# The last inverse-Haar pieces of two channel chunks tied behind the joins of the inverse stage, in half pieces

## The chip, the cores and the metric

The kernel runs on one core of a Trainium2 chip. The metric is the device time of one execution in microseconds (us). The core's engines are PE (TensorE, matrix products), DVE (VectorE), ACT (ScalarE), POOL (GpSimd) and SP (SyncE, which issues transfers). The page also has PEld, PE's loading of weights, which overlaps PE's products.

## The reference, cut to what matters

The input is four images (batches) of 64 channels with 256 x 256 points. Four layers follow each other. Layers 0, 1 and 3 are long convolutions with a filter that is a product of a row filter and a column filter, plus the input times a bias for each channel:

```python
k = jnp.einsum('ijk,imk->ijmk', hx, hy)[0]
...
y = jnp.fft.irfft2(u_f * k_f, s=(fft_size, fft_size))[..., :L, :L]
out = y + x * bias[:, None, None]
```

Layer 2 transforms each channel with a two-dimensional Haar transform, mixes the channels with soft thresholds, transforms back and adds its input:

```python
f1 = haar2d(x)
acc = jnp.zeros_like(f1[:, :conv_w.shape[1]])
for i in range(v.shape[0]):
    f3 = f1 * v[i]
    f4 = jnp.einsum('bchw,oc->bohw', f3, conv_w[i])
    f5 = jnp.sign(f4) * jax.nn.relu(jnp.abs(f4) - tau[i])
    acc = acc + f5
y = haar2d(acc, inverse=True)
return y + x
```

## The kernel before

A separable convolution of a channel is two matrix products with triangular Toeplitz matrices, one for the columns and one for the rows (`contract`, lines 262 to 266, four matmuls a product). For each batch b there are three kinds of work.

`convolutions` runs layers 0 and 1 for the 64 channels, one channel a tick: product a0, copy by ACT (line 279), product y0, residual sum by DVE (line 296), the same again for a1 and y1, and then the forward Haar transform. Its results go to memory, as coefficients (`coef`) and as row sums and differences (`keep`).

`mixing` runs 64 groups of four Haar rows: matmuls (line 453) into PSUM, scaling by DVE and ACT (lines 472 and 477), the soft threshold (lines 481 to 492), and a sum into the large tile `z` (line 498). `z` holds a whole batch after the mixing: 128 partitions, then four chunks of 16 channels, 128 Haar rows (slots), and four values for each channel.

`inverse` transforms back and runs layer 3. It begins three ticks after the 64 ticks of mixing, at the tick called `start`, and takes one channel a tick: `fetch` (ACT, line 538) copies the channel out of `z`, `rows` (PE, lines 545 and 546) transforms its rows into one of two PSUM buffers, `join` (DVE, lines 564 to 572) adds the row sums and differences in one operation (line 567) and writes the sum and the difference of the halves (lines 570 and 571) into a tile `u`. Product a3, its copy by ACT, product y3, residual sum by DVE (line 296) and the transfer of the output follow from `u`. In batches 0 to 2 every third channel (2, 5, 8 and so on) is put off: its `u` goes to memory and its layer 3 runs during the mixing of batch 3.

The inverse transform along the other axis is done in place in `z`. For chunk 0 it is a product with a Haar matrix (`halves` and `cols`, lines 549 to 562), in the first 16 ticks. For chunks 1 to 3 DVE does it by levels: `level` (lines 306 to 310) calls `halve` (lines 301 to 304), a subtraction (line 303) and a second operation (line 304), over pairs of slots. Level n has n pairs of slots of 64 values; levels 32 and 64 are cut into pieces of 16 pairs, which are operations of 128 x 1024. So each chunk has seven such pieces: one of level 16, two of level 32 and four of level 64. Piece (3, 64, 2) below is chunk 3, level 64, third piece; it needs the level before it and the mixing groups that write its slots, and `fetch` of the chunk's first channel (16 times the chunk's number) needs all pieces of the chunk.

Each step is put at a time in ticks by hand (`at`, and the table `PLACE`); all steps are then written into the program in the order of these times. The scheduler of the framework places each engine's instructions in this order of preference, but takes an instruction of a later time first where the engine would be free in its plan and the data are there. An order that it must keep is given with `add_manual_dep`. Such an order between two instructions of one engine needs no semaphore.

The pieces of chunk c (1 to 3) are written at `start + 16 (c - 1)` and the ticks after it (lines 583 to 591): (2, 64, 3) at `start + 28`, (3, 32, 0) and (3, 32, 1) at 34 and 36, (3, 64, 0) to (3, 64, 3) at 38, 40, 42 and 44.

## Time and profile before

| | us |
|---|---|
| Median of three runs | 2873.04 |
| Lowest and highest of the three | 2872.15, 2877.78 |
| The profiled execution | 2873.81 |
| Span of its instructions | 2871.9 |

The busy times on the page are unions of the instructions' times. A matmul's end is modelled and consecutive matmuls overlap, so PE's idle time says more than its busy time. The 40 slices of the page are 71.8 us each:

```profile
DVE  4555558999999779999999769999999779999985
PEclk9999999999999999999999999999999999999999
```

The digits are the busy share of a slice in tenths. DVE's slices of 9 are the mixing stages, and the pairs of lower digits between them are the inverse stages of batches 0, 1 and 2. Joins (line 567) of batch 0 run from 873.9 us on, those of batch 1 from 1530.4, of batch 2 from 2182.5 and of batch 3 from 2648.0. In batch 0, join 16 starts at 932.1, join 28 at 964.5 and join 40 at 996.2.

### The profile page before, as it was taken

To read this page: it belongs to the slowest core of one execution; us is meant where nothing else is said; L and a number is where in the kernel's file an instruction comes from. 1 tells how busy PE (TensorE), PEld (TensorE's weight loads), DVE (VectorE), ACT (ScalarE), POOL (GpSimd) and SP (SyncE) were. 2 spreads that over 40 slices of the span, in tenths; PEclk is the share of its full clock that TensorE was granted. 3 is DMA by queue.
4 is the path that set the end of the run, shared out by engine and by line. 5 is a ranking of instruction groups with operands and counts; after the bars stand their busy time and mean duration, and the time that the engine had idled before them with its cause. 6 is when DMAs were issued, how large, how long until landed. Compare 5 with 4: busy or idle time off the path is not lost.

```text
span 2871.9 us, 52418 instructions
## 1 busy us (share of the span) xinstructions
PE 2822.6 (98%) x16594; PEld 2553.8 (89%) x16594; DVE 2492.5 (87%) x4240; ACT 2078.6 (72%) x4941; POOL 334.0 (12%) x644
## 2 busy tenths in 40 slices
PE   9999999999998999999999999999999999999999
PEld 8899998888887998998888898998888998888998
DVE  4555558999999779999999769999999779999985
ACT  2333348999985658989986658999995659998554
POOL 0111111122121001221211001121121000000000
PEclk9999999999999999999999999999999999999999
DMA  6877787676676986777777976777777988777786
GB/s 195 249 229 233 230 237 219 207 211 204 204 212 220 284 248 199 214 212 213 208 212 236 295 247 195 216 212 215 211 208 232 301 267 237 228 238 213 223 241 199
DMA packets 599382, 649.77 MB, mean 226 GB/s; under 512 B 48481, under 2 KB 517060, under 8 KB 598980
## 3 DMA queue, kind: packets, MB, share of 16 engines
q1 hardware_dynamic: 537012, 578.61, 68.3%
q10 hardware_dynamic: 62096, 67.82, 6.7%
q8 instruction: 134, 2.20, 0.3%
q14 instruction: 140, 1.15, 0.1%
HBM read 426.77 MB, written 219.48 MB: 225 GB/s over the span
## 4 chain that ended last, share of the span: by engine, by line
PE 46%; DVE 12%; ACT 5%; issue 3%; DMA 2%; POOL 0%; SPq 0%; ACTq 0%; DVEq 0%
PE pa L265 11%; PE py L265 11%; PE px L453 6%; PE pa L266 5%; PE py L266 5%; PE pw L545 3%; ACT f L477 3%; DVE mag L492 2%; DVE y L296 2%; DVE mag L488 2%; PE pw L546 2%; DMA t<-pad 1%; PE pz L385 1%; DVE z L498 1%; ACT mag L481 1%
## 5 line engine op out<-in xcount | busy, mean ns | idle before, releaser
L265 PE MATMUL py<-t,a 128*128 128x256 f32 x3072 | 922.4, 382 | 12.1 <-ACT a L279 11.2
L279 ACT COPY a<-pa 128x512 f32<-128x512 f32 x768 | 479.9, 625 | 500.4 <-PE pa L266 455.2
L477 ACT ACTIVATE f<-px,vt 128x64 f32<-128x64 f32 x2816 | 613.1, 369 | 100.6 <-DVE f L472 99.8
L266 PEld LDWEIGHTS py<-t,a 128*128 128x128 f32 x3072 | 583.4, 190 | 79.3
L266 PE MATMUL py<-t,a 128*128 128x128 f32 x3072 | 590.0, 274 | 0.0
L265 PEld LDWEIGHTS py<-t,a 128*128 128x128 f32 x3072 | 497.2, 191 | 53.8 <-ACT a L279 21.6
L453 PE MATMUL px<-wb,f 128*128 128x256 f32 x2048 | 487.6, 380 | 7.6 <-ACT f L477 7.6
L453 PEld LDWEIGHTS px<-wb,f 128*128 128x128 f32 x2048 | 369.0, 190 | 50.1 <-ACT f L477 10.5
L355 POOL TENSOR_TENSOR sd<-less 128x128 f32<-128x128 f32 (+4 forms) x320 | 190.2, 594 | 1859.7 <-DVE less L354 1478.3
L538 ACT COPY zc<-z 128x512 f32<-128x512 f32 x256 | 281.8, 1104 | 108.6 <-PE pw L546 100.1
L488 DVE TENSOR_TENSOR mag<-mag,vt 128x1024 f32<-128x1024 f32 x256 | 311.8, 1218 | 12.7 <-ACT mag L481 12.1
L265 PE MATMUL pa<-t,y 128*128 128x256 f32 x1024 | 309.0, 384 | 8.5 <-DVE y L296 5.5
L492 DVE SCALAR_TENSOR_TENSOR mag<-mag,f 128x1024 f32<-128x1024 f32 x256 | 311.8, 1219 | 0.0
L265 PE MATMUL pa<-t,x 128*128 128x256 f32 x1024 | 305.9, 380 | 1.8 <-DMA t<-pad 1.8
L481 ACT ACTIVATE mag<-f 128x1024 f32<-128x1024 f32 x256 | 296.0, 1156 | 2.7 <-DVE z L498 0.4
L378 DVE TENSOR_TENSOR sp<-sd,sp 128x512 fp32r<-128x512 f32 x256 | 178.5, 697 | 128.8 <-ACT sp L373 127.5
L484 ACT ACTIVATE f<-f 128x1024 f32<-128x1024 f32 x256 | 285.9, 1117 | 3.5
L265 PE MATMUL pa<-t,u 128*128 128x256 f32 x772 | 233.2, 384 | 6.7 <-ACT w L552 2.8
L296 DVE SCALAR_TENSOR_TENSOR y<-x,bsb,py 128x512 f32<-128x512 f32 x256 | 189.9, 742 | 45.5 <-PE py L266 45.3
L266 PEld LDWEIGHTS pa<-t,y 128*128 128x128 f32 x1024 | 194.5, 190 | 26.4
L266 PEld LDWEIGHTS pa<-t,x 128*128 128x128 f32 x1024 | 194.6, 190 | 26.3
L296 DVE SCALAR_TENSOR_TENSOR y<-y,bsb,py 128x512 f32<-128x512 f32 x256 | 189.5, 740 | 26.0 <-PE py L266 25.6
(72 smaller groups left out, 4378.5 us busy)
## 6 DMA issues: line engine op xcount, KB each, us to landing
t<-pad SPq DMA_DIRECT2D x767, 256.0 KB, 4.1
x<-in_x SPq DMA_DIRECT2D x256, 256.0 KB, 3.7
coef<-co SPq DMA_DIRECT2D x256, 256.0 KB, 3.1
f<-coef SPq DMA_DIRECT2D x256, 256.0 KB, 3.2
r<-keep SPq DMA_DIRECT2D x256, 256.0 KB, 4.0
out_y<-y ACTq DMA_DIRECT2D x193, 256.0 KB, 4.2
keep<-sums SPq DMA_DIRECT2D x256, 128.0 KB, 2.9
keep<-sd SPq DMA_DIRECT2D x256, 128.0 KB, 2.8
```

The costliest lines, as they stand in the source:

```text
L265: nc.tensor.matmul(ps[:, m, :], src[:, 0, m * P : (m + 1) * P], t[:, ::-1], start=True, stop=False)
L266: nc.tensor.matmul(ps[:, m, P:], src[:, 1, m * P : (m + 1) * P], t[:, : P - 1 : -1], start=False, stop=True)
L279: nc.scalar.copy(a, s["p" + new])
L296: nc.vector.scalar_tensor_tensor(y, s[res], bsb[:, layer, c : c + 1], s["p" + new], ALU.mult, ALU.add)
L355: engine.tensor_tensor(t[:, :, :, half:length], v[..., 0], v[..., 1], ALU.subtract)
L453: nc.tensor.matmul(ps[:, q, h, :], f[:, q, h * P : (h + 1) * P], wb.rearrange("p r n -> p (r n)"), start=True, stop=True,)
L477: nc.scalar.mul(f4[:, j], px[:, j], scale(g, 0)[:, j : j + 1])
L481: nc.scalar.activation(mag, st[g]["f4"], AF.Abs)
L484: nc.scalar.activation(st[g]["f4"], st[g]["f4"], AF.Sign)
L488: nc.vector.tensor_sub(mag, mag, over(g, 1, 16))
L492: nc.vector.scalar_tensor_tensor(mag, mag, 0.0, st[g]["f4"], ALU.max, ALU.mult)
L538: nc.scalar.copy(a.rearrange("p h k i -> p (h k) i"), z[:, c // 16, :, :, c % 16].rearrange("p i x -> p x i"))
```

## The change

A table `LATE` names pieces by batch: seven in batch 0, four each in batches 1 and 2, none in batch 3. A piece in the table is cut into two halves of eight pairs (operations of 128 x 512), written at the two ticks that the table gives, and the first operation of each half may not be placed ahead of the first operation (line 567 before) of the join that was written last before it; a half at tick k so goes behind the join of channel k - 1. In batches 0 to 2 the pieces of chunk 3 that are not in the table are written 17 ticks earlier than before (`start + 15` in place of `start + 32`). All other pieces stay where they were.

```diff
--- before.py
+++ after.py
@@ -82,6 +82,21 @@
     "l add": 3.47,
 }
 
+LATE = (
+    {
+        (2, 64, 3): (21, 23),
+        (3, 32, 0): (18, 19),
+        (3, 32, 1): (25, 27),
+        (3, 64, 0): (28, 29),
+        (3, 64, 1): (31, 32),
+        (3, 64, 2): (34, 35),
+        (3, 64, 3): (37, 38),
+    },
+    {(2, 64, 3): (21, 23), (3, 64, 1): (24, 26), (3, 64, 2): (28, 31), (3, 64, 3): (34, 37)},
+    {(2, 64, 3): (21, 23), (3, 64, 1): (24, 26), (3, 64, 2): (28, 31), (3, 64, 3): (34, 37)},
+    {},
+)
+
 INV_2PI = float(np.float32(1.0 / (2.0 * math.pi)))
 MAGIC = float(1.5 * 2.0**23)
 
@@ -298,16 +313,20 @@
 
         return [product, residual]
 
-    def halve(even, odd):
-
-        nc.vector.tensor_sub(odd, even, odd)
+    behind = [None]
+
+    def halve(even, odd, stay=False):
+
+        first = nc.vector.tensor_sub(odd, even, odd)
+        if stay and behind[0] is not None:
+            tc.add_manual_dep(first.ins, behind[0].ins.name, order, reason="not ahead of the joins")
         nc.vector.scalar_tensor_tensor(even, even, 2.0, odd, ALU.mult, ALU.subtract)
 
-    def level(n, chunk, begin=0, count=None):
+    def level(n, chunk, begin=0, count=None, stay=False):
 
         count = n if count is None else count
         v = z.rearrange("p n s x c -> p n s (x c)")[:, chunk].rearrange("p (j e s) x -> p j e s x", e=2, s=P // 2 // n)
-        halve(v[:, begin : begin + count, 0, 0, :], v[:, begin : begin + count, 1, 0, :])
+        halve(v[:, begin : begin + count, 0, 0, :], v[:, begin : begin + count, 1, 0, :], stay)
 
     def butterfly():
 
@@ -564,7 +583,7 @@
         def join(c):
             ps = st[c]["pw"]
             t = io.tile([P, 2, 2, P], F32, name=f"t_{b}_{c}", tag="res", bufs=BUFS["res"])
-            nc.vector.scalar_tensor_tensor(t, st[c]["r"], 0.5, ps, ALU.mult, ALU.add)
+            behind[0] = nc.vector.scalar_tensor_tensor(t, st[c]["r"], 0.5, ps, ALU.mult, ALU.add)
             u = io.tile([P, 2, S], F32, name=f"u_{b}_{c}", tag="y", bufs=BUFS["y"])
             v = u.rearrange("p m (w e) -> p m w e", e=2)
             nc.vector.tensor_add(v[:, :, :, 0], t[:, 0], t[:, 1])
@@ -576,19 +595,25 @@
 
         along = start - groups - 3
 
-        def when(tick, n, chunk, *span):
-            at(tick + PLACE["level"], lambda _: level(n, chunk, *span), 0)
+        def when(tick, n, chunk, *span, stay=False):
+            at(tick + PLACE["level"], lambda _: level(n, chunk, *span, stay=stay), 0)
 
         at(along + 11 + PLACE["level"], lambda _: butterfly(), 0)
         for chunk in range(1, 4):
             turn = start + 16 * (chunk - 1)
             for n in (1, 2, 4, 8):
                 when(along + 12 + 3 * chunk if b + 1 < B else turn, n, chunk)
+            if chunk == 3 and b + 1 < B:
+                turn = start + 15
             when(turn + 1, 16, chunk)
-            for i in range(2):
-                when(turn + 2 + 2 * i, 32, chunk, 16 * i, 16)
-            for i in range(4):
-                when(turn + 6 + 2 * i, 64, chunk, 16 * i, 16)
+            for n in (32, 64):
+                for i in range(n // 16):
+                    tick = LATE[b].get((chunk, n, i))
+                    if tick is None:
+                        when(turn + n // 16 + (n == 64) * 2 + 2 * i, n, chunk, 16 * i, 16)
+                    else:
+                        for j in range(2):
+                            when(start + tick[j], n, chunk, 16 * i + 8 * j, 8, stay=True)
 
         for c in range(C):
             for name, stage in zip(("sooner", "early", "fetch", "rows"), (sooner, early, fetch, rows)):
```

## The prediction

> **What bounds the kernel now.** I read the busy line first, then the busy time by stretch around the inverse stage, then the waits of PE there, then the order of VectorE's instructions at the longest wait.

> ```profile
> PE 2822.6 (98%) x16594; PEld 2553.8 (89%) x16594; DVE 2492.5 (87%) x4240; ACT 2078.6 (72%) x4941; POOL 334.0 (12%) x644
> ```

> PE, the matrix engine, is busy nearly all the time, so only its remaining idle time and slow stretches can be won. By stretch (columns: length; busy PE, weight loads, DVE, ACT, POOL, with counts; PE clock granted, DMA share, GB/s):

> ```profile
> 840.00:937.00 97.00, 87.35 (x525) 77.66 (x524) 94.43 (x156) 55.31 (x90) 10.02 (x20) 0.98 0.71 221
> 932.20:936.50 4.30, 4.30 (x16) 3.82 (x17) 2.83 (x6) 0.59 (x1) 0.00 (x0) 0.60 0.95 308
> 936.00:961.00 25.00, 24.93 (x167) 23.10 (x167) 18.32 (x35) 14.34 (x18) 0.00 (x0) 0.99 0.84 266
> 961.00:993.50 32.50, 32.49 (x213) 29.38 (x212) 24.56 (x47) 21.12 (x28) 0.00 (x0) 1.00 0.96 296
> 1591.00:1613.00 22.00, 21.26 (x140) 19.20 (x139) 15.45 (x30) 13.56 (x18) 0.00 (x0) 1.00 0.90 292
> 1613.00:1644.00 31.00, 30.99 (x204) 28.05 (x203) 23.75 (x46) 19.53 (x26) 0.00 (x0) 1.00 0.96 296
> 2648.00:2746.00 98.00, 97.13 (x630) 89.65 (x630) 97.47 (x162) 51.87 (x69) 0.00 (x0) 1.00 0.74 223
> ```

> The first two lines are batch 0 where mixing ends and the inverse stage begins (joins 0 to 16): DVE is full (94.43 of 97.00) and PE idles 97.00 - 87.35 = 9.65 us. Right after (joins 17 to 39) PE idles 0.08 us and DVE has room: 25.00 - 18.32 = 6.68 and 32.50 - 24.56 = 7.94 us. Batch 1 has 6.55 and 7.25 us of room at the same joins. What PE waits for, in 840 to 937:

> ```profile
> PE pa L265 <- issue: 2.1, 1, 2.1
> PE pw L545 <- ACT zc L538: 2.0, 1, 2.0
> PE py L265 <- ACT a L279: 1.7, 2, 1.5
> PE pw L545 <- DVE w L553: 1.5, 1, 1.5
> PE pa L265 <- DVE y L296: 1.4, 1, 1.4
> PE pa L265 <- DVE u L571: 0.6, 2, 0.3
> PE pa L265 <- PE pw L546: 0.3, 1, 0.3
> ```

> The first is put down to "issue"; DVE's order shows the cause, and PE's timeline the end of the wait:

> ```profile
> 926.56 0.68 DVE L567 SCALAR_TENSOR_TENSOR t<-r,pu 128x512 f32<-128x512 f32 x1
> 927.16 1.21 DVE L303 TENSOR_TENSOR z<-z 128x1024 f32<-128x1024 f32 x1
> 928.29 0.41 DVE L570 TENSOR_TENSOR u<-t 128x256 f32<-128x256 f32 x1
> 928.63 0.41 DVE L571 TENSOR_TENSOR u<-t 128x256 f32<-128x256 f32 x1
> 928.96 1.21 DVE L304 SCALAR_TENSOR_TENSOR z<-z 128x1024 f32<-128x1024 f32 x1
> 930.10 0.68 DVE L567 SCALAR_TENSOR_TENSOR t<-r,pu 128x512 f32<-128x512 f32 x1
> ```
> ```profile
> 932.20 0.67 PE L265 MATMUL pa<-t,u 128*128 128x256 f32 x2 [2.14 <-issue]
> ```

> A level piece stands inside join 14 (L303 between L567 and L570) and its second half ahead of join 15, which ends at 932.10; 0.10 us later PE, idle since 930.06, goes on. L303 of the large shape runs eleven times in that stretch and never after 927.2 in this stage, although the last seven pieces are written at ticks 33 to 44: pieces are placed wherever DVE is free in the planned order. In batches 1 and 2 they have all run by the first join; there PE waits only this around it (1493 to 1560):

> ```profile
> PE pa L265 <- ACT w L552: 1.4, 1, 1.4
> PE pw L545 <- DVE w L553: 0.7, 1, 0.7
> ```

> **The change part by part.**

> Moved: 7 pieces in batch 0, 4 each in batches 1 and 2. A large op occupies DVE from 927.16 to 928.29, 1.13 us; the other from 928.96 to 930.10, 1.14; a piece is 2.27 us. Seven are 15.9 us, seven of the last eight of those eleven by written order (ticks 28 and 34 to 44), taken out of a stretch with 97.00 - 94.43 = 2.57 us of DVE room.

> Gain in batch 0. Of the waits I count those that a late DVE can make: 2.1 + 2.0 + 1.5 + 1.4 + 0.6 + 0.3 = 7.9 us; not the 1.7 behind ACT's copy. The 2.0 behind ACT's fetch is the doubtful one. Then the clock: 0.60 over the 4.30 us after the longest wait loses 0.4 x 4.30 = 1.7 us. Together 9.6. Batches 1 and 2, whose DVE holds no pieces after the first join, still lose 1.4 + 0.7 = 2.1 there, so I take 9.6 - 2.1 = 7.5 us. Bounds: 0 (the waits have other causes) and 9.6.

> [...]

> Gain in batches 1 and 2. The last pieces there run at 1527.48 and 1529.29 on DVE, directly ahead of the first join at 1530.43, for which PE waits 1.4 us; 2.27 us less brings that join earlier by more than the wait. The 0.7 is a queue of the same DVE work. 2.1 us each. Bounds: 0, and 2.1 + 2.1 (in the mixing stretch 1057 to 1493 PE waits 1.6 us for DVE's residual sums and 0.5 for ACT's copy). The rest of DVE's relief in mixing I cost at nothing, because PE is busy 433.22 of 435.60 us there: PE's own work hides it.

> Added: 30 instructions. A half op is 128x512; the nearest rows are L378 (same shape, 0.68 us, next start 0.61 later at 1515.70) and L567 above (next start 0.60 later). So a half piece is 1.20 us, a piece 2.40, 0.13 more than now, 15 x 0.13 = 2.0 us of DVE over the program, inside the room below.

> [...]

> Cost at ticks 18 to 38. A half tied at tick k goes behind join k - 1. Batch 0: five (18 to 25) are 6.0 us into 6.68 of room; nine (27 to 38) are 10.8 us into 7.94: DVE is 2.9 us over, and since joins feed PE within 0.1 us (row above) I let PE lose all 2.9. What is late next: join, product a3, then the rows, for which there are two PSUM buffers. The stretch after tick 39 (5.86 us of room in 26.5) lets DVE catch up, but not PE. Batches 1 and 2: four halves, 4.8 us, into 6.55 and four into 7.25: they fit, and I take 0.5 us each for joins that a half stands inside. Bounds for each half: 0 and its full 1.20 us on PE's path, so 0 to 36 us in all; the nearest row is batch 3 (2648 to 2746), where whole pieces stand between joins, DVE is busy 97.47 of 98.00 and PE loses only 0.87. So near the low end.

> The tie itself: an order on one engine, no semaphore. Behind a tied op in DVE's queue stand that join's two sums, the next join and residual sum; PE's a3 and ACT's output transfer wait for these. No transfer moves in any queue. The last half of chunk 3 comes at tick 38 and the first fetch (L538) of that chunk at 48, ten ticks of over 2 us: hidden; were DVE later than that, ACT would wait. Chunk 3's earlier untied pieces only change priority: 0. Batch 3: unchanged.

> Sum: batch 0 -7.5 + 2.9 = -4.6; batches 1 and 2 2 x (-2.1 + 0.5) = -3.2; together -7.8. The profiled execution took 2873.8 us (span 2871.9), 0.8 over the median of 2873.04; 2873.8 - 7.8 = **2866.0 us**.

> **Rivals.**

> A, the stall moves along (faster by too little). Every tied half stands inside its join, as L303 does at 927.16, and delays u by 0.6 us; in each group of three channels one is deferred and one join feeds PE with some 0.1 to 0.3 us to spare, so about 13 joins lose 0.4: 5.2 us in place of the two 0.5, on top of 2.9. 2866.0 + 4.2 = 2870.2. For: the row at 927.16. Against: at 979.09 L378 stands inside a join (L570 at 978.75, L571 at 979.69), and PE waits 0.2 us in all from 936 to 1057.

> B, slower: the rotation join, a3, rows breaks under the halves as it does now under whole pieces. Then seven pieces cost at ticks 18 to 38 what they cost now, 9.6, against the gain of 7.5: +2.1; and four pieces cost 9.6 x 4/7 = 5.5 in batches 1 and 2 against 2.1: +3.4 each. 2873.8 + 8.9 = 2882.7. It decides once DVE is over 0.97 busy at those joins. For: 10.8 us into 7.94. Against: batch 3's row, and DVE's share after the change at batch 1's joins 20 to 39, (15.45 + 23.75 + 9.6) / 53 = 0.92.

> C, more: all waits bounded above vanish. 9.6 + 2 x 4.2 = 18.0 less the cost of 3.9: 2859.7. For: DVE is the releaser of most. Against: some are ACT's.

> D, the tie does not do what it says: the pieces before the tied ones move up, into the freed DVE time, and the waits stay; 2873 us. Against: only four of the eleven are left.

> **How the numbers follow.** Forecast 0.50, own range 2860 to 2871 (batch 0's gain 9.6 or its cost doubled); A 0.15; B 0.18; C 0.13; D 0.04. About 0.2%, 5.7 us, can be told from no change here: faster means under 2867.3. Faster: 0.40 of the forecast, C, 0.01 of A, 0.54. Within: 0.10 of the forecast, 0.13 of A, D, 0.27. Slower: B and 0.01 of A, 0.19. The range 2856 to 2880 leaves out the far part of C and the upper half of B, some 0.14.

> **What will show it.** Right: DVE's large L303 ops gone between joins 1 and 15 of batch 0, PE's idle time in that stretch down from 9.65 to 2 or 3 us, no 0.60 clock; half-size ops between joins 17 and 38; DVE near 1.0 in batch 0 at joins 27 to 39 with some 3 us of PE idle time; the 1.4 us ahead of the first join gone in batches 1 and 2. Wrong: new waits of pa for u above 4 us in a batch (A, B), or the waits of joins 0 to 16 still there without the pieces (their cause was ACT or PSUM buffers).

## The result, and the profile after

| | before | after |
|---|---|---|
| Median, six runs each, us | 2873.24 | 2858.89 |
| Lowest and highest, us | 2872.15, 2877.78 | 2858.58, 2860.41 |
| The profiled execution, us (span) | 2873.81 (2871.9) | 2858.95 (2857.1) |

The ratio is 0.995 (95% interval 0.9938 to 0.9962): 14.4 us faster. Timed again (e5), the ratio was 0.997 (0.9958 to 0.9981), 9.9 us between the medians of 2872.23 and 2862.32. Both intervals end below 1.

The line of busy times of the changed kernel:

```profile
PE 2820.0 (99%) x16594; PEld 2552.1 (89%) x16594; DVE 2492.0 (87%) x4270; ACT 2076.4 (73%) x4941; POOL 329.1 (12%) x644
```

The sums are those of before; DVE has the 30 added instructions and no more time. In what follows an inverse stage runs from the last mixing matmul of its batch to the first of the next. The stretches of batch 0's inverse stage, cut at joins 17 and 40, in the kernel before (columns: length; busy PE, weight loads, DVE, ACT, POOL; PE clock, DMA share, GB/s):

```profile
839.50:933.70 94.20, 84.55 (x514) 75.20 (x514) 93.48 (x155) 55.22 (x90) 10.02 (x20) 1.00 0.71 220
933.70:996.20 62.50, 62.43 (x404) 57.05 (x404) 46.40 (x89) 37.74 (x48) 0.00 (x0) 0.98 0.91 284
```

and the same stretches in the changed kernel, with the rest of the stage:

```profile
837.60:925.20 87.60, 83.70 (x522) 75.80 (x520) 78.82 (x142) 55.80 (x91) 9.09 (x20) 1.00 0.76 232
925.20:986.10 60.90, 60.18 (x391) 54.30 (x390) 59.64 (x116) 37.65 (x48) 0.00 (x0) 1.00 0.90 283
986.10:1048.10 62.00, 62.00 (x423) 57.97 (x422) 45.59 (x89) 32.37 (x40) 0.00 (x0) 1.00 0.92 290
```

Up to join 17 DVE has 14.7 us less to do, the stretch is 6.6 us shorter, and PE's idle time falls from 9.65 to 3.90 us. From there to join 40 DVE is now full (59.64 of 60.90), yet PE idles only 0.72 us. PE's waits in the changed kernel, first up to join 17, then to join 40:

```profile
PE py L280 <- ACT a L294: 1.7, 2, 1.5
PE pw L564 <- ACT zc L557: 1.2, 1, 1.2
PE pw L564 <- ACT w L571: 1.0, 1, 1.0
```
```profile
PE pw L564 <- DVE t L586: 0.4, 1, 0.4
PE pw L564 <- ACT zc L557: 0.2, 1, 0.2
```

Of the waits that were shown before, the one of 2.1 us behind a join, the 1.5 for DVE's halves and the 1.4 for a residual sum are gone; the 1.7 for ACT's copy is as it was. Of the 2.0 us behind ACT's fetch 1.2 are left, and a wait of 1.0 us for ACT's copy `w` (line 571) is new. A half piece among the joins (lines 586, 589 and 590 are the join; 320 and 323 the piece; 311 the residual sum; 397 part of the forward transform):

```profile
960.08 0.69 DVE L586 SCALAR_TENSOR_TENSOR t<-r,pw 128x512 f32<-128x512 f32 x1
960.69 0.69 DVE L320 TENSOR_TENSOR z<-z 128x512 f32<-128x512 f32 x1
961.29 0.42 DVE L589 TENSOR_TENSOR u<-t 128x256 f32<-128x256 f32 x1
961.63 0.42 DVE L590 TENSOR_TENSOR u<-t 128x256 f32<-128x256 f32 x1
961.96 0.69 DVE L397 TENSOR_TENSOR sp<-sd,sp 128x512 fp32r<-128x512 f32 x1
962.57 0.68 DVE L323 SCALAR_TENSOR_TENSOR z<-z 128x512 f32<-128x512 f32 x1
```

It does stand inside its join, and holds L589 until 961.29; without a piece, L570 of before started 0.72 us after its L567 (943.15 and 943.87 in the trace of before), so here by 960.80. The price is 0.49 us.

### The profile page after: what moved, and what is told of

It reads as the page before. It is cut to its first block, busy times and chain, and to the rows that moved or that the text cites. A ratio compares the mean times of both kernels' runs of the same rounds, so it can differ in the third digit from the quotient of the medians.

```text
span 2857.1 us, 52492 instructions
## 1 busy us (share of the span) xinstructions
PE 2820.0 (99%) x16594; PEld 2552.1 (89%) x16594; DVE 2492.0 (87%) x4270; ACT 2076.4 (73%) x4941; POOL 329.1 (12%) x644
## 5 line engine op out<-in xcount | busy, mean ns | idle before, releaser
L472 PEld LDWEIGHTS px<-wb,f 128*128 128x128 f32 x2048 | 369.0, 190 | 50.5 <-ACT f L496 10.8
```

Source lines behind the costliest of these rows:

```text
L472: nc.tensor.matmul(ps[:, q, h, :], f[:, q, h * P : (h + 1) * P], wb.rearrange("p r n -> p (r n)"), start=True, stop=True,)
```

## The experiments

The stage lengths from the traces say more than the times, because they repeat. In us; a mixing stage is the stretch between two inverse stages:

| kernel | inverse 0 | inverse 1 | inverse 2 | first stage |
|---|---|---|---|---|
| before | 217.9 | 216.8 | 209.2 | 440.1 |
| before, again (e1) | 217.5 | 213.5 | 209.8 | 438.3 |
| after | 210.5 | 212.3 | 208.4 | 437.7 |
| after, again (e2) | 210.6 | 212.4 | 208.4 | 442.0 |
| after, a third time (e5) | 210.5 | 213.4 | 208.4 | 439.4 |
| batch 0 only (e3) | 210.7 | 214.1 | 209.3 | 437.3 |
| batches 1 and 2 only (e4) | 217.5 | 212.3 | 208.4 | 441.4 |
| halves, not tied (e6) | 212.9 | 214.7 | 209.8 | 439.0 |
| whole pieces, tied (e7) | 216.3 | 213.8 | 210.4 | 442.2 |
| tied behind the join's last op (e8) | 211.7 | 212.7 | 208.9 | 437.5 |
| two more pieces moved (e9) | 212.5 | 212.3 | 208.4 | 440.8 |
| quarters (e10) | 212.5 | 212.1 | 208.3 | 439.4 |
| all pieces of batches 0 to 2 halved (e11) | 211.0 | 212.5 | 208.8 | 440.5 |
| batch 3's halved too (e12) | 210.7 | 212.4 | 208.6 | 437.8 |

Some expectations speak of "PE's loss over steady pace": the sum of how much later than at full pace each matmul starts after the one ahead of it (full pace is taken as 216 ns after a matmul of 256 columns, 110 after one of 128; the medians from start to next start in the trace of before are 216 and 111). It holds PE's idle time and some 3 us a stretch of matmuls that start late by little.

**e1 and e2, both kernels again.** No edit.

> The kernel before, unchanged, profiled a second time. In its first profile PE lost 2.6 us at 118 us (a Toeplitz load in the first stage) and 2 x 1.2 us in batch 1's inverse stage, where ACT's issue of the output transfer took 1.8 and 2.0 us; the changed kernel's profile has 0.9 us and none. Theory (these belong to each execution, not to the change): in this second profile they are elsewhere or gone, and the span stays within 2870 to 2876 us. Rival (they belong to the planned order of the kernel before, and the change removed them): they come again at the same places with the same lengths.

> The changed kernel, unchanged, profiled a second time. Theory (chance waits): first stage 437 to 441 us, batch 1's inverse stage 212 to 216 us, depending on where transfers are slow; batch 0's inverse stage stays at 210.5 us and DVE is again 0.93 to 1.00 busy at joins 16 to 39 of batch 0 with PE idle about 1 us. Rival (all differences are the change's): every stage repeats within 0.3 us.

The kernel before took 2867.75 us this time, below the range given. The long issues of the output transfer in batch 1 were gone (its stage 213.5 in place of 216.8 us), with one of 1.17 us in batch 2, and PE's wait at 118 us had become one of 1.4 us at 116. In the changed kernel the first stage took 442.0 us in place of 437.7 (I had said up to 441), and its inverse stages repeated within 0.1. So the first stage and the long issues vary with the execution, in either kernel: over all profiles the first stage lies between 437.3 and 442.2 us, and issues of the output transfer of more than 1 us came three times in the first profile of before, once in e1, three times in e6, once in e7, once in a third profile of the changed kernel (e5) and never in its first two. That the change makes the long issues rarer is not excluded: of the five profiles whose batches 1 and 2 have no tied halves (before, e1, e3, e6, e7) four hold at least one, of the nine others one. What surely belongs to the change lies in the inverse stages.

**e3 and e4, one part alone.** In e3 the table and the new `turn` hold for batch 0 only, in e4 for batches 1 and 2 only:

```diff
-            if chunk == 3 and b + 1 < B:
+            if chunk == 3 and b == 0:
```

> Only batch 0's pieces are moved, tied and halved. Theory: the gain of each batch lies in its own inverse stage and they add: batch 0's stage 217.9 to 210.5 us, so about 2866 us (2873.2 - 7.4). Rival (much of the total comes from batches 1 and 2): 2869 us or more.

> Only the pieces of batches 1 and 2 are moved, tied and halved. Theory (batch 1's long waits for output transfers are chance, the change gives 0.8 to 1.2 us a batch, as its profile shows in batch 2): 2871 to 2872 us. Rival (the change removes them too): 4.5 + 0.8 = 5.3 us, 2868 us. My forecast's term for these two batches was 3.2 us, 2870 us.

e3: 2863.66 us, ratio 0.9974 (0.9964 to 0.9984). e4: 2866.36 us, ratio 0.9986 (0.9977 to 0.9994); before in the same session 2870.26. Each kernel has the short stages of the batches that it changes and the long ones of the others, so the gains add: 7.0 us in batch 0 (217.5 to 210.5), 1.2 to 1.8 in batch 1 (213.5 and 214.1 to 212.3) and 0.8 to 1.4 in batch 2, together 9 to 10 us. The medians of e4 say 3.9 us where the stages say 2 to 3; its interval (1.7 to 6.6 us) holds both.

**e5, the changed kernel timed again.** No edit.

> The changed kernel again, timed. By stage the change is worth 6.5 us in batch 0 and 1.4 and 1.1 us in batches 1 and 2, 9.0 to 9.5 us; the rest of the 14.4 us measured first is waits that come and go with the execution. Theory: ratio 0.9965 to 0.997, some 9.5 us. Rival (the change also makes the chance waits rarer, as in the first six runs of it, which lay within 1.8 us): 14 us again, ratio 0.995.

Ratio 0.997 (0.9958 to 0.9981), 9.9 us by the medians: the theory. The interval reaches from 5.5 to 12.1 us, so 14 us again is out, but a part of the rival (rarer waits) is not. The first measurement's 14.4 us holds some 4 to 5 us that the stages don't show as the change's. In the first pair of profiles 2.4 us are the first stage and 3.3 batch 1's stage with its two long issues (216.8 in place of 213.5); that its six runs fell so is not explained further.

**e6, halves without the tie.**

```diff
-                            when(start + tick[j], n, chunk, 16 * i + 8 * j, 8, stay=True)
+                            when(start + tick[j], n, chunk, 16 * i + 8 * j, 8)
```

> The changed kernel without the ties: the same half pieces at the same ticks, free to be placed earlier. The planned order puts them at joins 0 to 22 of batch 0 and at joins 0 and 1 of batches 1 and 2. Theory (where the work stands sets the time, not its size or its written tick): batch 0's inverse stage 215 to 218 us, batches 1 and 2 213.5 and 209.3 as before, 2869 to 2873 us. Rival (halving alone relieves the joins, because a half holds a join by 0.6 instead of 1.2 us): batch 0 at 212 us or less, 2865 us.

The number of my theory fell: the halves ran up to join 22 of batch 0, as planned, and its stage took 212.9 us, 4.6 us less than with whole pieces (217.5 in e1). The rival's 212 us was missed by 0.9. 2864.43 us, ratio 0.9972 (0.9962 to 0.9982), which the time alone can't tell from the changed kernel. The stretches up to join 17 and to join 40:

```profile
837.90:929.40 91.50, 85.65 (x525) 76.30 (x524) 90.58 (x161) 56.38 (x91) 8.94 (x20) 1.00 0.74 226
929.40:990.00 60.60, 60.43 (x394) 54.93 (x394) 49.12 (x96) 36.14 (x47) 0.00 (x0) 1.00 0.93 295
```

DVE is as full up to join 17 as before (90.58 of 91.50), but PE idles 5.85 us there in place of 9.65. This is not the gain of halving in place. The whole pieces had all run by join 14; here six operations of halves stand behind join 17, so DVE has 2.9 us less to do up to there and the stretch is 2.7 us shorter. The other 1.9 us of the gain are in the second stretch (60.60 in place of 62.50), where the kernel before lost most of 1.7 us to a slow clock (*The clock* below) and this one loses none. So untied halves find places farther back, and what a half relieves where a whole piece stood is not measured here. Batches 1 and 2, where halves and whole pieces alike run around the first joins, come nearer to that: up to join 17 they take 90.6 us in place of 91.2. Their stages (214.7 and 209.8 us) are no shorter than before; each holds one long issue of the output transfer (1.9 and 1.65 us).

**e7, whole pieces with the tie.**

```diff
-                        for j in range(2):
-                            when(start + tick[j], n, chunk, 16 * i + 8 * j, 8, stay=True)
+                        when(start + tick[0], n, chunk, 16 * i, 16, stay=True)
```

> The changed kernel with whole pieces, tied at the first of each piece's two ticks (joins 18 to 37). Theory (DVE's room is what counts; in batch 3 whole pieces between joins cost PE 0.9 us in 98): joins 17 to 39 of batch 0 lose at most 1 us more than with halves (PE's loss over steady pace there 4.0 us with halves), the whole within 1.5 us of the changed kernel. Rival (a whole op of 1.13 us inside a join holds u longer than its 0.1 to 0.3 us of lead): some 0.9 us for each of the 7 + 8 pieces at a join that feeds PE, 5 us in batch 0 and 3 each in batches 1 and 2, about 2871 us.

The rival: 2870.84 us, ratio 0.9996 (0.9986 to 1.0005), no gain that can be measured. Against the changed kernel the stages are 5.8, 1.5 and 2.0 us longer, where it had 5, 3 and 3. The same stretches as above, and PE's waits in the second:

```profile
841.20:928.80 87.60, 83.73 (x523) 75.89 (x521) 78.85 (x142) 55.76 (x91) 9.07 (x20) 1.00 0.75 231
928.80:995.50 66.70, 61.49 (x392) 54.69 (x391) 59.97 (x103) 36.44 (x47) 0.00 (x0) 1.00 0.84 261
```
```profile
PE py L280 <- ACT a L294: 3.2, 5, 0.7
PE pa L280 <- DVE u L590: 1.9, 4, 0.6
```

The first stretch is that of the changed kernel to 0.03 us of PE's busy time; the second is 5.8 us longer, with 5.21 us of idle PE in place of 0.72, although DVE has less share of work (59.97 of 66.70). Nine waits, none over 0.7 us: not a shortage of DVE, but single operations of 1.13 us that hold a join whose `u` PE is about to read. Product y3 waits for ACT's copy because that copy waits for the product from the late `u`: three of the five waits for the copy stand 2.25 us behind a wait for `u` (962.49 behind 960.24, 971.94 behind 969.69, 981.40 behind 979.15).

**e8, tied behind the join's last operation.**

```diff
-            behind[0] = nc.vector.scalar_tensor_tensor(t, st[c]["r"], 0.5, ps, ALU.mult, ALU.add)
+            nc.vector.scalar_tensor_tensor(t, st[c]["r"], 0.5, ps, ALU.mult, ALU.add)
...
-            nc.vector.tensor_sub(v[:, :, :, 1], t[:, 0], t[:, 1])
+            behind[0] = nc.vector.tensor_sub(v[:, :, :, 1], t[:, 0], t[:, 1])
```

> The changed kernel with each half tied behind the last operation of its join, not the first, so that no half can stand inside the join that it is tied to. Rival A of my prediction in small (a half inside a join delays u and so PE): the new waits of PE at joins 17 to 39 (0.62 us for u in batches 1 and 2 at join 30, about 1.3 us in batch 0) go. Theory (the halves fill time in which the join's next operation could not start yet, and hold it by little): stage lengths the same within 0.5 us.

The waits for `u` did go, as the rival says, but nothing was won: batch 0 is 1.2 us longer (211.7), batches 1 and 2 0.4 and 0.5. From join 17 to join 40 of batch 0 PE waits 1.1 us for operation t of a join in place of 0.4, and in batches 1 and 2 0.5 us for t in place of 0.5 for `u`. That a half which may not use the pause inside its own join holds up the next one instead fits this, and is not shown further.

**e9, two more pieces.**

```diff
-        (2, 64, 3): (21, 23),
+        (2, 64, 1): (18, 20),
+        (2, 64, 2): (22, 24),
+        (2, 64, 3): (26, 27),
```

> The changed kernel with two more pieces of batch 0, (2, 64, 1) and (2, 64, 2), tied in halves at ticks 18 to 24, and (2, 64, 3) at 26 and 27: nine pieces in place of seven at joins 17 to 40, 4.8 us more of DVE where DVE has 0.02 x 61 = 1.2 us of room. Theory (halves cost PE nothing while DVE has room, the excess costs in full): PE's loss at joins 17 to 40 rises from 4.0 to 7 or 8 us, and the loss up to join 17 falls from 7.5 to about 6. Rival (the room limit doesn't bind, DVE's queue makes it good after join 40): 4.0 to 5 us, and the stage is shorter than 210.5 us.

The theory: PE's loss went from 4.0 to 8.1 us from join 17 to join 40, and fell from 7.5 to 5.5 up to join 17. Second stretch and its longest waits:

```profile
925.30:990.30 65.00, 61.01 (x391) 54.59 (x391) 64.26 (x124) 37.54 (x48) 0.00 (x0) 1.00 0.85 265
```
```profile
PE pw L566 <- DVE t L588: 3.1, 4, 1.5
```

DVE is busy 64.26 of 65.00, and 4.8 us more work made the stretch 4.1 us longer. Here DVE's room does bind: the seven pieces of the change fill it just to the edge.

**e10, quarters.**

```diff
-                            when(start + tick[j], n, chunk, 16 * i + 8 * j, 8, stay=True)
+                            for q in range(2):
+                                when(start + tick[j] + 0.5 * q, n, chunk, 16 * i + 8 * j + 4 * q, 4, stay=True)
```

> The changed kernel with each tied half cut again into two quarters (128 x 256, about 0.41 us), at the same joins. Whole pieces cost PE 9.7 us at joins 17 to 40 of batch 0 and 5.0 in batches 1 and 2, halves 4.0 and 3.3. Theory (what counts is how long one op can hold a join): quarters 3 to 4 us and 3 us, a small further gain, unless their added DVE time (0.34 x 2 - 0.60 = 0.08 us an op, 28 ops, 2.2 us in batch 0, where there is 1.2 of room) takes it back: then 5 us in batch 0 and 3 us in batches 1 and 2. Rival (halves won for another reason, a place in the planned order): no order by size, batches 1 and 2 off by more than 0.5 us.

5.5 us of loss in batch 0 and 3.1 to 3.2 in batches 1 and 2. Where DVE has no room the added time costs: the stage of batch 0 was 2 us longer. Where it has room the stages were 0.2 and 0.1 shorter than the changed kernel's, where the changed kernel's own differ by up to 0.1 from profile to profile, and the mixing stages of these batches were 0.3 and 0.2 us longer (435.7 and 435.5). So the small gain is not shown.

**e11 and e12, all pieces halved.** e11 halves the pieces of levels 32 and 64 that the table doesn't name, in batches 0 to 2, without a tie; e12 in batch 3 too:

```diff
-                        when(turn + n // 16 + (n == 64) * 2 + 2 * i, n, chunk, 16 * i, 16)
+                        for j in range(2):
+                            count = 8
+                            when(turn + n // 16 + (n == 64) * 2 + 2 * i, n, chunk, 16 * i + 8 * j, count)
```

> The changed kernel with all pieces of levels 32 and 64 of batches 0 to 2 halved, also those that run in the mixing stages, not tied. Theory (short ops hold the joins and residual sums less): batch 0 up to join 17 from 7.5 to 6 us or less, batches 1 and 2 there 3.9 to 3.5, mixing stages the same or 1 us shorter: 1 to 3 us faster than the changed kernel. Rival (DVE is 0.97 to 0.98 busy in the mixing stages, and 0.13 us a piece more there makes it the bound): mixing stages 1 us longer each, no gain.

> As the kernel with all pieces halved in batches 0 to 2, and batch 3's pieces of levels 32 and 64 halved too, not tied. Theory (a whole piece costs only where the join it holds has no spare time ahead of PE; in batch 3 deferred channels give PE other work, and PE loses 0.9 us in 98 with whole pieces between the joins): batch 3's stages 271.6 and 246 us as before within 1 us, 2855 us again. Rival (halves win wherever pieces meet joins): batch 3's inverse stage 3 us or more shorter, 2852 us.

e11: 2855.31 us, ratio 0.9938 (0.9925 to 0.9952). The size of the theory came, and more, but in another place: not up to join 17 but in the mixing stages, 397.2 us in batch 0 (399.0 to 399.9 before and after) and 434.4 in batches 1 and 2 (435.2 to 435.4), some 4 us in all. Why they became shorter is not worked out. e12: **2851.11 us**, ratio 0.9935 (0.9922 to 0.9949) to 2869.47 in its session, the fastest of the kernels here. Batch 3's mixing stage and inverse stage, first in the changed kernel, then in e12:

```profile
2339.50:2611.00 271.50, 264.93 (x1435) 236.79 (x1434) 266.27 (x390) 258.64 (x678) 0.00 (x0) 1.00 0.79 231
2611.00:2857.10 246.10, 237.48 (x1545) 219.26 (x1543) 201.78 (x341) 126.78 (x171) 0.00 (x0) 1.00 0.73 219
```
```profile
2335.20:2605.50 270.30, 264.27 (x1435) 236.50 (x1434) 265.09 (x391) 258.55 (x678) 0.00 (x0) 1.00 0.79 232
2605.50:2849.60 244.10, 236.68 (x1545) 219.15 (x1543) 204.15 (x377) 126.14 (x171) 0.00 (x0) 1.00 0.74 220
```

3.2 us less together, with DVE busier in the inverse stage by 2.4 us: the rival, in its direction. The ratios of e11 and e12 overlap, so that e12 beats e11 is shown by the stages (in e11 batch 3's are 271.6 and 246.5 us), not by the time.

## Why the prediction was right, and where it was not

The time, 2858.89 us, lies in the range, and the direction was right. The size was 7.8 us against 14.4 measured first, 9.9 measured again, and 9 to 10 by the stages.

*Batch 0's gain, 7.5 us:* right. The stretch up to join 17 became 6.6 us shorter (94.20 to 87.60). Of the waits that I had counted 1.2 us are there still, behind ACT's fetch, and 1.0 us behind ACT's `w` is new: 2.2 us, where I had taken 2.1 off. The idle time fell by 5.75 us, and the 1.7 us of the slow clock went too, together 7.45. That it agrees so closely is partly luck, because the 2.1 were read off other waits, in batches 1 and 2. e7, with the same work taken out of that stretch and whole pieces, has the same 87.60 us, so it is the move that wins them.

*Batch 0's cost at ticks 18 to 38, 2.9 us:* too large; PE's idle time there rose from 0.07 to 0.72 us. This is nearly all of the 2.4 us by which batch 0's 4.6 fell short of 7.0. I had cut the ticks into two windows and let the second overfill by 2.9, as if all of DVE's other work had to stay in its window. DVE's busy time from join 17 to join 40 rose by only 59.64 - 46.40 = 13.2 us for 14 x 1.20 = 16.8 us of halves: some 3.6 us of its other work ran outside these joins. That DVE at its limit does cost in full is shown by e9: 4.8 us more work, with 1.2 us of room for it, made the stretch 4.1 us longer.

*The reason I gave for a low cost fell.* "The nearest row is batch 3, where whole pieces stand between joins ... So near the low end": whole pieces at these joins cost PE 5.21 us of idle time (e7), and e12 shows that they were not free in batch 3 either. The step that I costed at 0.13 us a piece and no gain, the halving, is what makes the move cheap. By batch 0's stage, from 217.5 us: the move of whole pieces gives 1.2 us (e7), the same move in halves 7.0, so that halving is worth 5.8 at these places. (The 4.6 us of e6 are not halving alone, since its halves stand farther back than the whole pieces did.) My bound of 0 to 1.20 us for each half was on the right mechanism, but I did not price a whole piece by the same rows, and so named as the change's worth only where the pieces stand, and not also how long one of them can hold a join.

*Batches 1 and 2, 1.6 us each:* 1.2 to 1.8 and 0.8 to 1.4. The 1.4 us ahead of the first join and the 0.7 behind it are gone; a wait of 0.7 us for ACT's fetch took their place. The mixing stages, costed at nothing, kept their 435.4 us.

*The clock, 1.7 us:* right in size, but not tied to the longest wait alone, as I had it. A wait of the same 2.12 us stands in e1 and e4, whose batch 0 is the old one; the 4.3 us after it ran at 0.62 of the clock in e1 and at 1.00 in e4:

```profile
929.90:934.20 4.30, 4.24 (x16) 3.84 (x17) 2.90 (x6) 0.59 (x1) 0.00 (x0) 0.62 0.97 333
```
```profile
935.30:939.60 4.30, 4.27 (x27) 3.91 (x28) 3.11 (x7) 1.68 (x4) 0.00 (x0) 1.00 0.98 339
```

But e4 has its slow stretch elsewhere in the same stage, behind the 2.0 us wait for ACT's fetch:

```profile
873.50:876.90 3.40, 1.39 (x11) 1.10 (x10) 3.40 (x8) 3.19 (x5) 0.00 (x0) 1.00 0.44 146
876.90:880.30 3.40, 3.40 (x13) 3.04 (x14) 3.34 (x5) 1.10 (x1) 0.00 (x0) 0.50 0.25 77
```

*Rival A* (a half inside its join) happens, at 0.49 us in the row shown, but PE's waits for `u` at these joins are one of 0.5 us each in batches 1 and 2, and none in batch 0's list. Placed after the join instead, the halves cost more (e8). *Rival B* (the rotation breaks) is nearest to what whole pieces do (e7), at a smaller price: 5.21 us of idle PE where B had 9.6. *Rival C*, 2859.7 us, is nearest to the first time, but not for its reason: the mixing stages gave nothing. *D* is refuted: the pieces that stayed did not move up, and their waits did not stay.

## What to carry to other kernels

Where one engine's queue mixes short links of a chain with long work that nobody waits for, ask how long one piece of that work can hold the next link, and not only how full the engine is: moved whole, the pieces gave back all but 1.2 of the 7.0 us that the same move won in halves, and a half costs the engine only some 0.07 us more than its share of a whole. Move filler work to a stretch that has room for it as a whole, and stop when the room is used (two pieces more than fit lost 2 us). Compare stages that the change touches, profile by profile: the changed kernel's repeat to 0.1 us where no long issue falls into them, those of before to 0.6, while the first stage alone varies by 5 us.

## What the hardware showed that I had not expected

ACT's issue of an output transfer, 0.38 us at 1595.06 in the trace of before, took 1.0 to 2.0 us up to three times in an execution, in either kernel, and PE waited up to 1.2 us for the copy that stood behind it in ACT's queue; why is left open. The same 2.1 us wait of PE was followed by a clock of 0.60, 0.62 and 1.00 in three executions; what the seven slow stretches have in common is 2.0 us or more of idle PE inside the one window of 3.41 us ahead of them. In the first stage four of the fourteen profiles have such a stretch, between 118 and 124 us, behind a wait that stands there in most of them.
